# A four-layer graph network on one core: the start re-ordered, the last z kept on chip, the last part spread over four engines

## The chip, the cores and the metric

One core of a Trainium2 chip. The time is device microseconds (us) of one execution, the median of several; most executions of a kernel agree within 0.3%. "The profile" is one execution recorded by the hardware profiler; stages are compared by when their first or last TensorE record starts, read to 0.1 us, so that a difference can be 0.1 off. TensorE does the matrix products and writes them to PSUM, one of the two on-chip memories; the other is SBUF. VectorE, ScalarE and GpSimd do the element-wise work, SyncE and GpSimd issue most transfers.

## The reference

Four graph layers on x of shape (128, 128, 256) in fp32: 128 graphs of 128 nodes, 256 features. Every layer ends in a layer norm over the features.

```python
# _L0: edge attention; _L1: three graph convolutions 256->512->1024->256; _L2: three products
x = _layernorm(x + _L0_gnn_ref(x, ...))
x = _layernorm(x + _L1_gnn_ref(x, ...))
x = _layernorm(x + _L2_gnn_ref(x, ...))
# _L3, cut to what matters: batch norms over ALL 128*128 rows
h   = relu(_batchnorm(agg.reshape(-1, d) @ W1.T + b1, g1, be1))   # z before the norm: 512 wide
out = _batchnorm(h @ W2.T + b2, g2, be2)
x = _layernorm(x + out.reshape(b, n, -1))
```

A batch norm over all rows is a barrier: no row can pass it before the last row's statistics are there. There are two, so the kernel has a loop (layers 0 to 2 and the first product of layer 3), then the second product (the last stage), then the last part (second batch norm applied, addition, layer norm, store).

## The kernel before

The 128 graphs are taken as 32 quads of four. A start fills the software pipeline, a loop runs the quads, and two blocks follow. z (1 MB per quad) and x3, the input of the last addition, are parked in DRAM.

```python
# start (cut): issue order is program order
nc.sync.dma_start(w1_sb, ...)
nc.sync.dma_start(att_dram[0]..., zero)            # 1 MB of zeros
nc.sync.dma_start(w2_sb, ...)                      # 2 MB
...                                                # project quad 0, store its rows
quads[0].xr = load_x(0, "xr", 3, wk)               # 0.5 MB
...                                                # sort the edge index
nc.sync.dma_start(att_dram[1]..., zero)            # 1 MB of zeros
for c in range(NE): score(0, c)                    # score reads the gathered rows
gather(1, [...])                                   # GpSimd: rows of quad 1
... attention(0); scatter(0)                       # GpSimd: attention to DRAM, then loaded back
... stage_a(0)                                     # py: first products with the attention matrix
score(1, NE - 1); values_in(3, xg3); ... softmax of quad 1 ...
attention(1); scatter(1)
mix1(0, 0); mix1(0, 2); first(0, ...); mix2(0, ...)
```

```python
# the end of the loop, and after it (cut)
if c == K3 - 1:
    nc.sync.dma_start(z_dram[k], s.zt...)          # every z goes to DRAM
...
for q in range(NQ):                                # last stage
    z = wk.tile([P, K3, QB * N], F32, tag="zl", bufs=4)
    nc.sync.dma_start(z, z_dram[q]...)
    ... ReLU of the batch norm on ScalarE, 16 matmuls, statistics ...
for q in range(NQ):                                # last part
    nc.sync.dma_start(x3, x3_dram[q]...)
    for o in range(DC): nc.scalar.activation(ag[:, o, :], ...)      # scale and shift
    for j in range(0, QB, 2):
        ... four transposes on TensorE into PSUM ...
        nc.vector.tensor_add(x3[:, j:j + 2, :], x3[:, j:j + 2, :], pt)
        layer_norm(wk, x3[:, j:j + 2, :])          # statistics and both applications on VectorE
    nc.scalar.dma_start(out[...], x3)
```

## Time and profile before

3448.07 us median of 3 runs (3447.54 to 3450.75); profiled span 3446.5.

| stage, by the start of TensorE records | us |
|---|---|
| first product with an attention matrix (py) | 81.8 |
| first large matmul (second convolution of quad 0) | 126.4 |
| last product of the loop (hidden) | 3069.7 |
| first product of the last stage (po) | 3080.6 |
| last product of the last stage | 3301.8 |
| end | 3446.5 |

First a window of the last part. Columns: stretch, its length, then busy us and instructions of TensorE, its weight loads, VectorE, ScalarE and GpSimd, then the granted TensorE clock, the DMA share and GB/s.

```profile
3350.00:3360.00 10.00, 5.31 (x23) 4.17 (x21) 10.00 (x40) 7.76 (x14) 0.00 (x0) 0.50 0.83 254
```

VectorE is full, GpSimd unused, and TensorE at half clock. Then GpSimd's order of events in the start: the gather of quad 1's rows and the first two scatters of quad 0's attention (start, duration, what; in brackets how long the engine had waited, and for what).

```profile
46.62 0.97 POOL L184 DMA_INDIRECT z<-qd,src_idx  x1 [0.30 <-issue]
...
64.16 1.02 POOL L240 DMA_INDIRECT attd<-at,att_idx  x1 [3.97 <-DVE at L234]
67.97 1.01 POOL L240 DMA_INDIRECT attd<-at,att_idx  x1 [2.80 <-DMA attd<-at,att_idx]
```

And TensorE in the end of the start:

```profile
98.46 1.02 PE L206 MATMUL pe<-ident,es 128*16 128x128 f32 x4 [7.36 <-DVE es L199]
99.27 9.58 PE L168 MATMUL pq<-wqv,xt 128*128 128x512 f32 x16
...
111.57 3.50 PE L284 MATMUL pm<-wt_t,xr 128*128 128x128 f32 x16
```

A wait of 7.36 us for edge scores stands ahead of all further work.

### The profile page before, as it was taken

Reading aid. Unit: us, or ns where it says so; the run is one execution under the profiler, and the core shown is the slowest. Engines: PE = TensorE matmul, PEld = TensorE weight load, DVE = VectorE, ACT = ScalarE, POOL = GpSimd, SP = SyncE. Lnnn points to the kernel's source line nnn. Section 1 sums busy time; section 2 is a strip of 40 time slices with the busy share of each in tenths; the row PEclk is TensorE's granted clock in tenths of the full one; section 3 lists DMA queues with packets and bytes.
Section 4 is the critical chain, followed back from the end, with each engine's and each line's share of the span. In section 5 each row is a group of like instructions: output and inputs, shape, how many; then the busy total and the mean of one; then the engine's idle time right before and its main releaser. Section 6 shows DMA issues by size and latency. Waiting matters only on the chain.

```text
span 3446.5 us, 33811 instructions
## 1 busy us (share of the span) xinstructions
PE 3294.4 (96%) x13134; PEld 2102.9 (61%) x13134; DVE 1754.5 (51%) x3522; ACT 979.9 (28%) x1655; POOL 570.1 (17%) x463
## 2 busy tenths in 40 slices
PE   5899999999999999999999999999999999989963
PEld 3566666666666666666666666666666666654442
DVE  6554455544555455455554455545545553233379
ACT  2222222222222222222222222222222222224452
POOL 4211122222221111112122222211111220000000
PEclk7899999999999999999999999999999999999975
DMA  8412333333332322233333333233223331034446
GB/s 259 124 63 73 92 98 99 98 98 86 98 98 80 98 87 79 74 86 98 98 99 98 86 98 98 82 97 90 81 71 87 95 92 37 19 140 163 155 140 220
DMA packets 128015, 348.04 MB, mean 101 GB/s; under 512 B 14576, under 2 KB 68720, under 8 KB 115312
## 3 DMA queue, kind: packets, MB, share of 16 engines
q0 software_dynamic: 41088, 135.29, 16.6%
q1 hardware_dynamic: 65168, 191.58, 15.4%
q10 hardware_dynamic: 21600, 19.02, 1.7%
q8 instruction: 103, 1.69, 0.2%
q14 instruction: 56, 0.46, 0.0%
HBM read 258.82 MB, written 87.03 MB: 100 GB/s over the span
## 4 chain that ended last, share of the span: by engine, by line
PE 93%; DVE 4%; DMA 2%; issue 0%; ACT 0%; POOL 0%; DVEq 0%; POOLq 0%; ACTq 0%; SPq 0%
PE ph L318 26%; PE p L329 13%; PE po L377 10%; PE po L736 6%; PE ph L416 6%; PE ph L298 6%; PE pq L168 6%; PE po L273 3%; PE pm L308 3%; PE pm L363 3%; PE py L264 2%; PE pm L284 2%; PE pa L402 2%; PE po L340 2%; DVE x3l L98 1%; DVE x3l L755 1%
## 5 line engine op out<-in xcount | busy, mean ns | idle before, releaser
L318 PE MATMUL ph<-m,w 128*128 128x512 f32 x2048 | 884.2, 592 | 0.8 <-DVE m L309 0.8
L318 PEld LDWEIGHTS ph<-m,w 128*128 128x128 f32 x2048 | 389.0, 190 | 477.1 <-issue 474.5
L329 PE MATMUL p<-w,h 128*128 128x256 f32 x2048 | 450.4, 381 | 0.0
L184 POOL DMA_INDIRECT zs<-qd,src_idx x124 | 149.9, 1209 | 1729.6 <-DMA qd<-qt 1677.2
L329 PEld LDWEIGHTS p<-w,h 128*128 128x128 f32 x2048 | 386.6, 190 | 52.6 <-issue 0.5
L377 PE MATMUL po<-l2w,ms 128*128 128x256 f32 x1536 | 347.5, 379 | 1.2 <-DVE ms L369 1.2
L321 ACT ACTIVATE h<-ph 128x512 f32<-128x512 f32 x256 | 152.8, 597 | 592.6 <-PE ph L318 592.6
L377 PEld LDWEIGHTS po<-l2w,ms 128*128 128x128 f32 x1536 | 284.3, 190 | 36.1 <-DVE ms L369 1.4
L298 PE MATMUL ph<-w,mx 128*128 128x512 f32 x512 | 235.6, 593 | 0.0
L168 PE MATMUL pq<-wqv,xt 128*128 128x512 f32 x512 | 230.5, 603 | 2.2 <-ACT xt L156 2.2
L736 PE MATMUL po<-zl,l3w 128*128 128x512 f32 x512 | 221.8, 596 | 10.4 <-ACT zl L731 10.4
L416 PE MATMUL ph<-ag,l3w 128*128 128x512 f32 x512 | 225.5, 593 | 0.3 <-ACT ag L405 0.3
L184 POOL DMA_INDIRECT zs<-qd,dst_idx x124 | 192.5, 1553 | 143.8 <-DMA zs<-qd,src_idx 130.1
L342 DVE TENSOR_TENSOR xr<-xr,po 128x512 f32<-128x512 f32 x64 | 43.7, 683 | 338.3 <-PE po L340 338.3
L90 ACT ACTIVATE ln_sd<-ln_mv,eps 128x2 f32<-128x2 f32 x256 | 75.4, 294 | 461.9 <-DVE ln_mv L85 456.7
L240 POOL DMA_INDIRECT attd<-at,att_idx x128 | 128.2, 1001 | 417.9 <-DMA attd<-at,att_idx 283.9
L156 DVE COPY xt<-pt 128x512 f32<-128x512 f32 x58 | 37.4, 686 | 279.9 <-PE pt L154 279.9
L736 PEld LDWEIGHTS po<-zl,l3w 128*128 128x128 f32 x512 | 97.9, 191 | 134.3 <-issue 110.8
L416 PEld LDWEIGHTS ph<-ag,l3w 128*128 128x128 f32 x512 | 96.8, 190 | 121.7 <-issue 112.4
L98 DVE TENSOR_SCALAR xr<-xr,ln_mv,ln_rs 128x256 f32<-128x256 f32 x384 | 163.2, 467 | 6.9
L168 PEld LDWEIGHTS pq<-wqv,xt 128*128 128x128 f32 x512 | 96.5, 194 | 112.6 <-issue 109.1
L309 DVE COPY m<-pm 128x512 f32<-128x512 f32 x128 | 88.3, 690 | 147.2 <-PE pm L308 147.2
(176 smaller groups left out, 4013.9 us busy)
## 6 DMA issues: line engine op xcount, KB each, us to landing
ad<-attd SPq DMA_DIRECT2D x32, 1024.0 KB, 4.8
zd<-z SPq DMA_DIRECT2D x32, 1024.0 KB, 7.9
zl<-zd SPq DMA_DIRECT2D x32, 1024.0 KB, 4.8
xg<-in_x_dram SPq DMA_DIRECT2D x32, 512.0 KB, 4.4
xr<-in_x_dram SPq DMA_DIRECT2D x32, 512.0 KB, 5.8
x3d<-xr SPq DMA_DIRECT2D x32, 512.0 KB, 2.9
x3l<-x3d SPq DMA_DIRECT2D x32, 512.0 KB, 4.9
out_dram<-x3l ACTq DMA_DIRECT2D x32, 512.0 KB, 3.4
```

The lines of the kernel that those rows point to most:

```text
L98: nc.vector.tensor_scalar(r[:, i, :], r[:, i, :], mv[:, i, 0:1], rs[:, i:i + 1], op0=ALU.subtract, op1=ALU.mult)
L168: nc.tensor.matmul(pq, s.xts[i // 2][:, i % 2, c, :], wqv[:, c, :], start=(c == 0), stop=(c == DC - 1))
L184: nc.gpsimd.indirect_dma_start(out=s.z[c], out_offset=None, in_=s.qd, in_offset=bass.IndirectOffsetOnAxis(ap=idx[:, c:c + 1], axis=0), com ...
L240: nc.gpsimd.indirect_dma_start(out=ad, out_offset=bass.IndirectOffsetOnAxis(ap=att_idx[:, c:c + 1], axis=0), in_=s.at[:, c, :], in_offset= ...
L273: nc.tensor.matmul(po[:, t, :], yts[j // 2][:, t, dc, :], wo[:, dc, :], start=(dc == 0), stop=(dc == DC - 1))
L298: nc.tensor.matmul(ph, s.mx[i // 2 * 2][:, i % 2, dc, :], w1_sb[:, dc, :], start=(dc == 0), stop=(dc == DC - 1))
L318: nc.tensor.matmul(ph, w2_sb[:, c, f * P:(f + 1) * P], s.m2[:, c].rearrange("p b n -> p (b n)"), start=(c == 0), stop=(c == K1 - 1))
L321: nc.scalar.activation(h.rearrange("p b n -> p (b n)"), ph, AF.Relu)
L329: nc.tensor.matmul(p3[:, t * D:(t + 1) * D], s.h2[f][:, j + t, :], w3_sb[:, f, :], start=(f == 0), stop=(f == K2 - 1))
L377: nc.tensor.matmul(po[:, i % 2, :], mss[i][:, t, dc, :], l2w[:, t, dc, :], start=(n3 == 0), stop=(n3 == 3 * DC - 1))
L416: nc.tensor.matmul(ph, l3w1[:, dc, c * P:(c + 1) * P], s.ag[:, dc, :], start=(dc == 0), stop=(dc == DC - 1))
L736: nc.tensor.matmul(po, w2t[:, c, o * P:(o + 1) * P], z[:, c, :], start=(c == 0), stop=(c == K3 - 1))
```

## The change

Three intents. **Start:** three loads (w2, one xr, one zero fill, 3.5 MB) are issued later so that the first gather is not stuck behind them, and independent feed-forward work is put ahead of the softmax of quad 1. **Seam:** the last quad's z stays on chip over the first batch norm and is used first, while the other z come in; loads of small constants move to GpSimd. **Last part:** VectorE gives away what others can do. ScalarE applies the layer norm, for half the rows straight from PSUM. For these rows TensorE also does the scaling (a product with a diagonal matrix) and adds x3 (a product with the identity); GpSimd adds the shift to those x3 rows ahead of it and issues the stores.

```diff
-            nc.sync.dma_start(w2_sb, ...)                    # in the head of the start
-            quads[0].xr = load_x(0, "xr", 3, wk)
...
+            xg3 = load_x(3, "xg", 2)                         # behind the second index sort
+            nc.sync.dma_start(w2_sb, ...)
+            quads[0].xr = load_x(0, "xr", 3, wk)
             nc.sync.dma_start(att_dram[1]..., zero)
-            xg3 = load_x(3, "xg", 2)
... end of the start: values of quad 3 first, then score(1), mixes, first(0, 0) between the
... softmax steps of quad 1, and attention(1), scatter(1) last
... loop's last pass: third_mix between the halves of third; aggregation by halves
-            if c == K3 - 1:
+            if k == NQ - 1:
+                kept["z"] = s.zt
+            elif c == K3 - 1:
                 nc.sync.dma_start(z_dram[k], ...)
...
     with ExitStack() as phase:
+        bufs = phase.enter_context(tc.tile_pool(name="bufs", bufs=1))   # 14 large buffers
         cst = phase.enter_context(tc.tile_pool(name="cst3", bufs=1))    # constants
...
-            nc.scalar.dma_start(t, ap...)                    # b, gamma, beta
+            nc.gpsimd.dma_start(t, ap...)
...
+        order = [NQ - 1] + list(range(NQ - 1))
... last part, per quad
+                nc.scalar.activation(ag[:, o, :2 * N], ...)             # two, halves only
+                nc.gpsimd.tensor_add(x3s[q][:, 2:, :], x3s[q][:, 2:, :], shift_bc...)
+                        if j < 2: nc.tensor.transpose(...)
+                        else:     nc.tensor.matmul(dst_ps, a_in, diag2[:, o, :], ...)
+                nc.tensor.matmul(pt[1], ident, x3s[q][:, 2:, :], start=False, stop=True)
+                    mvs[q] = wk.tile([P, QB, 2], F32, tag="mv3", ...)   # mean and variance
+                    nc.vector.tensor_add(x3s[q][:, :2, :], x3s[q][:, :2, :], sums[q][0])
+                nc.vector.scalar_tensor_tensor(nm, mvs[q][:, :, 0], -1.0, rs, ...)  # the product
+                for i in range(QB): nc.scalar.activation(x3s[q][:, i, :], src_, ...)
+                nc.gpsimd.dma_start(out[...], x3s[q])
```

More of the change, by code (lines that the diff above doesn't have):

```diff
@@ L75, in gnn_stack @@
     st1 = ctile([P, K3, NQ, 6], "st1")
+    zpool = ctx.enter_context(tc.tile_pool(name="zpool", bufs=1))
+    kept = {}
     def norm_stats(pool, r):
@@ L322, in second, with third @@
             s.h2.append(h)
-        def third(k, j):
+        def third(k, j, between=None):
             s = quads[k]
@@ L327, in third @@
             for t in range(2):
+                if t and between:
+                    between()
                 for f in range(K2):
@@ L398, in stage_f @@
             ag = wk.tile([P, DC, QB * N], F32, tag="ag", name="ag", bufs=1)
-            for dc in range(DC):
-                pa = ps("pa")
-                for i in range(QB):
-                    nc.tensor.matmul(pa[:, i * N:(i + 1) * N], s.xr[:, i, dc * P:(dc + 1) * P], ahat_t,
+            pas = [ps("pa") for _ in range(DC)]
+            for i0, dc in ((i0, dc) for i0 in range(0, QB, 2) for dc in range(DC)):
+                for i in (i0, i0 + 1):
+                    nc.tensor.matmul(pas[dc][:, i * N:(i + 1) * N], s.xr[:, i, dc * P:(dc + 1) * P], ahat_t,
                                      start=True, stop=True)
+            for dc, pa in enumerate(pas):
                 if dc == 0:
@@ L412, in hidden @@
             if c == 0:
-                s.zt = wk.tile([P, K3, QB * N], F32, tag="z", name="z", bufs=1)
+                s.zt = zpool.tile([P, K3, QB * N], F32, tag="z", name="z", bufs=1)
             ph = ps("ph3")
@@ L475, in iteration @@
                 third(c, 0)
-                third(c, 2)
-                third_mix(c, 0)
                 if has_b:
+                    third(c, 2)
+                    third_mix(c, 0)
                     mix1(b, 0)
-                third_norm(c, 0)
+                    third_norm(c, 0)
+                else:
+                    third(c, 2, lambda: third_mix(c, 0))
+                    third_norm(c, 0)
                 third_mix(c, 2)
@@ L527, in start @@
                                         accum_out=rank[:, c:c + 1])
-            perm = wk.tile([P, NE, E], F32, tag="m2", name="perm", bufs=1)
+            perm = w2_sb[:, :2, :].rearrange("p c f -> p (c f)").rearrange("p (c e) -> p c e", c=NE)
             for c in range(NE):
@@ L541, in start @@
             nc.sync.dma_start(att_dram[0][:N * N, :].rearrange("(t s) r -> t (s r)", s=N), zero)
-            nc.sync.dma_start(w2_sb, w2.rearrange("(c p) f -> p c f", p=P))
             values_in(0, xg0, nc.scalar.copy)
@@ L596, in start @@
                 nc.vector.tensor_scalar(rs, kp, 1.0, BIG, op0=ALU.subtract, op1=ALU.mult)
+            xg3 = load_x(3, "xg", 2)
+            nc.sync.dma_start(w2_sb, w2.rearrange("(c p) f -> p c f", p=P))
+            quads[0].xr = load_x(0, "xr", 3, wk)
             nc.sync.dma_start(att_dram[1][:N * N, :].rearrange("(t s) r -> t (s r)", s=N), zero)
-            xg3 = load_x(3, "xg", 2)
             for c in range(NE):
@@ L605, in start @@
                     nc.vector.tensor_copy(log_col, pc[:, :, 1])
-            z2 = wk.tile([P, 2, QB * D], F32, tag="z", name="z_1", bufs=1)
+            z2 = zpool.tile([P, 2, QB * D], F32, tag="z", name="z_1", bufs=1)
             gather(1, [z2[:, 0, :], z2[:, 1, :], wk.tile([P, QB * D], F32, tag="xb", name="xb_1", bufs=1),
@@ L665, in start @@
             stage_a(0)
+            values_in(3, xg3)
+            for i in range(QB):
+                values(3, i)
             score(1, NE - 1)
-            values_in(3, xg3)
-            steps = softmax_parts(1)
-            for i in range(QB):
-                next(steps)
-                values(3, i)
-            for _ in steps:
-                pass
-            attention(1)
-            scatter(1)
             mix1(0, 0)
             mix1(0, 2)
+            steps = softmax_parts(1)
             first(0, 0)
+            next(steps)
             for i in range(QB):
@@ L682, in start @@
                 mix2(0, i)
+                next(steps, None)
+            attention(1)
+            scatter(1)
         with tc.manual_schedule(engines=None):
@@ L696, in vec @@
             t = ctile([P, n], name, pool=cst)
-            nc.scalar.dma_start(t, ap.rearrange("(c p) -> p c", p=P))
+            nc.gpsimd.dma_start(t, ap.rearrange("(c p) -> p c", p=P))
             return t
+        b1, g1, be1 = (vec(n, ap, K3) for n, ap in (("b1", l3_b1), ("g1", l3_g1), ("be1", l3_be1)))
         w2t = ctile([P, K3, D], "l3w2", pool=cst)
-        nc.scalar.dma_start(w2t, l3_w2_t.rearrange("(c p) f -> p c f", p=P))
-        b1, g1, be1 = (vec(n, ap, K3) for n, ap in (("b1", l3_b1), ("g1", l3_g1), ("be1", l3_be1)))
+        nc.gpsimd.dma_start(w2t, l3_w2_t.rearrange("(c p) f -> p c f", p=P))
         b2, g2, be2 = (vec(n, ap, DC) for n, ap in (("b2", l3_b2), ("g2", l3_g2), ("be2", l3_be2)))
@@ L724, in gnn_stack @@
         sc1, sh1 = batch_norm(st1, K3, b1, g1, be1, "n1")
-        outs = []
-        for q in range(NQ):
-            z = wk.tile([P, K3, QB * N], F32, tag="zl", name="zl", bufs=4)
-            nc.sync.dma_start(z, z_dram[q].rearrange("p (c n) -> p c n", c=K3))
-            for c in range(K3):
-                nc.scalar.activation(z[:, c, :], z[:, c, :], AF.Relu, bias=sh1[:, c:c + 1], scale=sc1[:, c:c + 1])
-            ag = keep.tile([P, DC, QB * N], F32, tag=f"agg{q}", name=f"agg{q}")
-            for o in range(DC):
-                po = ps("po3")
-                for c in range(K3):
-                    nc.tensor.matmul(po, w2t[:, c, o * P:(o + 1) * P], z[:, c, :],
-                                     start=(c == 0), stop=(c == K3 - 1))
-                nc.vector.bn_stats(st2[:, o, q, :], po)
-                nc.vector.tensor_copy(ag[:, o, :], po)
-            outs.append(ag)
@@ L741, in gnn_stack @@
-        sc2, sh2 = batch_norm(st2, DC, b2, g2, be2, "n2")
-        for q in range(NQ):
-            x3 = wk.tile([P, QB, D], F32, tag="x3", name=f"x3l{q}", bufs=7)
-            nc.sync.dma_start(x3, x3_dram[q].rearrange("p (b d) -> p b d", b=QB))
-            ag = outs[q]
-            for o in range(DC):
-                nc.scalar.activation(ag[:, o, :], ag[:, o, :], AF.Identity, bias=sh2[:, o:o + 1],
-                                     scale=sc2[:, o:o + 1])
-            for j in range(0, QB, 2):
-                pt = ps("pt3").rearrange("p (b d) -> p b d", d=D)
-                for t in range(2):
-                    for o in range(DC):
-                        nc.tensor.transpose(pt[:, t, o * P:(o + 1) * P], ag[:, o, (j + t) * N:(j + t + 1) * N], ident)
-                nc.vector.tensor_add(x3[:, j:j + 2, :], x3[:, j:j + 2, :], pt)
-                layer_norm(wk, x3[:, j:j + 2, :])
-            nc.scalar.dma_start(out[q * QB:(q + 1) * QB].rearrange("b n d -> n b d"), x3)
+        NB = 14
@@ new lines, in buf, with load_z @@
+        def buf(name):
+            return bufs.tile([P, 2 * QB * N], F32, tag="buf", name=name, bufs=NB)
+        def load_z(q):
+            if q == NQ - 1:
+                return [kept["z"][:, 2 * h:2 * h + 2, :] for h in range(2)]
+            z = [buf(f"zl{q}_{h}").rearrange("p (c n) -> p c n", c=2) for h in range(2)]
+            zq = z_dram[q].rearrange("p (c n) -> p c n", c=K3)
+            for h in range(2):
+                nc.sync.dma_start(z[h], zq[:, 2 * h:2 * h + 2, :])
+            return z
@@ new lines, in gnn_stack, with spread, load_x3, scaled @@
+        order = [NQ - 1] + list(range(NQ - 1))
+        outs = {}
+        with tc.manual_schedule(engines=None):
+            for q in order:
+                z = load_z(q)
+                for c in range(K3):
+                    zc = z[c // 2][:, c % 2, :]
+                    nc.scalar.activation(zc, zc, AF.Relu, bias=sh1[:, c:c + 1], scale=sc1[:, c:c + 1])
+                ag = keep.tile([P, DC, QB * N], F32, tag=f"agg{q}", name=f"agg{q}", bufs=1)
+                for o in range(DC):
+                    po = ps("po3")
+                    for c in range(K3):
+                        nc.tensor.matmul(po, w2t[:, c, o * P:(o + 1) * P], z[c // 2][:, c % 2, :],
+                                         start=(c == 0), stop=(c == K3 - 1))
+                    nc.vector.bn_stats(st2[:, o, q, :], po)
+                    nc.vector.tensor_copy(ag[:, o, :], po)
+                outs[q] = ag
+            sc2, sh2 = batch_norm(st2, DC, b2, g2, be2, "n2")
+            diag2 = ctile([P, DC, P], "diag2", pool=cst)
+            shift_bc = ctile([P, D], "shift_bc", pool=cst)
+            ones = ctile([P, P], "ones3", pool=cst)
+            nc.gpsimd.memset(ones, 1.0)
+            def spread():
+                wide = ctile([P, DC, P], "wide", pool=cst)
+                for o in range(DC):
+                    nc.vector.tensor_scalar(wide[:, o, :], ident, sh2[:, o:o + 1], None, op0=ALU.mult)
+                    nc.vector.tensor_scalar(diag2[:, o, :], ident, sc2[:, o:o + 1], None, op0=ALU.mult)
+                pr = ps("shift_ps")[:, :D]
+                nc.tensor.matmul(pr, ones, wide.rearrange("p o n -> p (o n)"), start=True, stop=True)
+                nc.vector.tensor_copy(shift_bc, pr)
+            x3s, sums, mvs, coefs = {}, {}, {}, {}
+            def load_x3(q):
+                x3s[q] = buf(f"x3l{q}").rearrange("p (b d) -> p b d", b=QB)
+                nc.sync.dma_start(x3s[q], x3_dram[q].rearrange("p (b d) -> p b d", b=QB))
+            def scaled(q):
+                ag = outs[q]
+                for o in range(DC):
+                    nc.scalar.activation(ag[:, o, :2 * N], ag[:, o, :2 * N], AF.Identity, bias=sh2[:, o:o + 1],
+                                         scale=sc2[:, o:o + 1])
+                if q == 0:
+                    spread()
+                nc.gpsimd.tensor_add(x3s[q][:, 2:, :], x3s[q][:, 2:, :], shift_bc.unsqueeze(1).to_broadcast([P, 2, D]))
+                pt = [ps("pt3").rearrange("p (b d) -> p b d", d=D) for _ in range(2)]
+                for j in range(QB):
+                    for o in range(DC):
+                        dst_ps, a_in = pt[j // 2][:, j % 2, o * P:(o + 1) * P], ag[:, o, j * N:(j + 1) * N]
+                        if j < 2:
+                            nc.tensor.transpose(dst_ps, a_in, ident)
+                        else:
+                            nc.tensor.matmul(dst_ps, a_in, diag2[:, o, :], start=(j == 2 and o == 0), stop=False,
+                                             skip_group_check=True)
+                nc.tensor.matmul(pt[1], ident, x3s[q][:, 2:, :], start=False, stop=True, skip_group_check=True)
+                sums[q] = pt
+            def moments(q, half):
+                if half == 0:
+                    mvs[q] = wk.tile([P, QB, 2], F32, tag="mv3", name="mv3", bufs=3)
+                    moments.st = wk.tile([P, QB, 6], F32, tag="st3", name="st3", bufs=2)
+                    nc.vector.tensor_add(x3s[q][:, :2, :], x3s[q][:, :2, :], sums[q][0])
+                src_ = x3s[q][:, :2, :] if half == 0 else sums[q][1]
+                for t in range(2):
+                    nc.vector.bn_stats(moments.st[:, 2 * half + t, :], src_[:, t, :])
+                for t in range(2):
+                    nc.vector.bn_aggr(mvs[q][:, 2 * half + t, :], moments.st[:, 2 * half + t, :])
+            def coefficients(q):
+                rs = wk.tile([P, QB], F32, tag="rs3", name="rs3", bufs=2)
+                nm = wk.tile([P, QB], F32, tag="nm3", name="nm3", bufs=2)
+                nc.vector.reciprocal(rs, coefs[q])
+                nc.vector.scalar_tensor_tensor(nm, mvs[q][:, :, 0], -1.0, rs, op0=ALU.mult, op1=ALU.mult)
+                coefs[q] = (rs, nm)
+            def apply(q):
+                rs, nm = coefs[q]
+                for i in range(QB):
+                    src_ = x3s[q][:, i, :] if i < 2 else sums[q][1][:, i - 2, :]
+                    nc.scalar.activation(x3s[q][:, i, :], src_, AF.Identity, bias=nm[:, i:i + 1], scale=rs[:, i:i + 1])
+                nc.gpsimd.dma_start(out[q * QB:(q + 1) * QB].rearrange("b n d -> n b d"), x3s[q])
+            for q in range(NB - 1):
+                load_x3(q)
+            scaled(0)
+            for q in range(NQ + 1):
+                if q < NQ:
+                    moments(q, 0)
+                if q + 1 < NQ:
+                    scaled(q + 1)
+                if q > 0:
+                    coefficients(q - 1)
+                    apply(q - 1)
+                    if q + NB - 2 < NQ:
+                        load_x3(q + NB - 2)
+                if q < NQ:
+                    moments(q, 1)
+                    sd = wk.tile([P, QB], F32, tag="sd3", name="sd3", bufs=2)
+                    nc.scalar.activation(sd, mvs[q][:, :, 1], AF.Sqrt, bias=eps)
+                    coefs[q] = sd
```

## The prediction

> **What bounds the kernel now.** I read the page's busy slices first, then the list of who waited for whom on TensorE, then the chain that ended last, then the ends of the span in small windows and instruction by instruction.
>
> ```profile
> PE   5899999999999999999999999999999999989963
> DVE  6554455544555455455554455545545553233379
> PEclk7899999999999999999999999999999999999975
> ```
>
> Forty slices of 86 us. TensorE is full from about slice 3 to slice 37, at full clock: that is the loop over quads (93.2 us each in the chain) and the first half of layer 3 (221.8 us for 512 matmul records). The diff changes none of those matmuls, so some 3200 of 3446 us cannot move. Only the ends can: the first slice and a half, the seam near 3070 us, and the last slice and a half, where VectorE is full and TensorE is not.
>
> ```profile
> PE pt L754 <- DVE ln_mv L85: 47.9, 22, 2.2
> PE pe L206 <- DVE es L199: 24.4, 2, 17.0
> PE py L264 <- ACT adc L250: 10.8, 1, 10.8
> PE po L736 <- ACT zl L731: 10.4, 1, 10.4
> PE pa L402 <- DVE xr L98: 2.4, 1, 2.4
> PE pm L363 <- DVE xr L98: 1.8, 1, 1.8
> ```
>
> TensorE's own waits (total us, times, longest): the last part's transposes behind VectorE, two waits for edge scores in the first 100 us (17.0 and 7.4), one for the first attention matrix, one for the first z of the last stage. The other rows of this list are at most 5.5 us.
>
> ```profile
> 3070.89 3.83 DMA zd<-z
> 3074.87 4.76 DMA zl<-zd
> 3080.61 221.80 PE po L736 x512
> ```
>
> The chain at the seam: store the last z, then load z again, then matmuls.
>
> ```profile
> L83 DVE BATCH_NORM_STATS2 ln_st<-x3l 128x6 f32<-128x256 f32 x128 | 50.2, 400 | 0.0
> L748 ACT ACTIVATE agg<-agg,n2shift,n2scale 128x512 f32<-128x512 f32 x64 | 47.5, 799 | 0.8 <-DVE n2shift L721 0.8
> L98 DVE TENSOR_SCALAR x3l<-x3l,ln_mv,ln_rs 128x256 f32<-128x256 f32 x128 | 44.1, 400 | 0.1
> L755 DVE TENSOR_TENSOR x3l<-x3l,pt 128x512 f32<-128x512 f32 x64 | 41.5, 652 | 2.5 <-PE pt L754 2.5
> L85 DVE BATCH_NORM_AGGREGATE ln_mv<-ln_st 128x2 f32<-128x6 f32 x128 | 19.8, 161 | 0.0
> 3427.60 0.15 DVE L85 BATCH_NORM_AGGREGATE ln_mv<-ln_st 128x2 f32<-128x6 f32 x1
> 3431.78 0.15 DVE L85 BATCH_NORM_AGGREGATE ln_mv<-ln_st 128x2 f32<-128x6 f32 x1
> ```
>
> The groups from 3303 us on, and one instruction of the same place in two successive quads: 4.18 us per quad, VectorE never idle. 32 x 4.18 = 134, with some 6 us of batch norm and start and 4 us of last store this is the 144 us from the last matmul (3302.4) to the end.
>
> **What the Trainium skill says.** "ScalarE: Activation LUTs", section What ACT_TABLE_LOAD costs: 186 ns + 0.833 ns per element, 93 ns more for each per-partition pointer operand, and back-to-back instructions overlap by 93 ns. The trace agrees: 186 + 2 x 93 + 427 = 799 ns, and the mean above is 799; three in a row took 2.21 us, so one each 0.705. For 256 columns with scale and bias this gives 585 ns, 492 ns apart (an estimate from that page). "TensorE: Matmul & The Clock Gate", section What's actually happening: the clock halves after an idle window of about 3.4 us and returns after a busy one. The trace agrees: granted clock 0.50 nearly throughout the last part, where TensorE was under 55% busy; 0.77 and then 1.00 just after 3308 to 3312 us, the 4 us in which it was wholly busy. "DMA: Bandwidth & Descriptors", section Issuing engines are not separate DMA queues: all queues share the same 16 engines. In the trace the first store of projected rows landed after 7.1 us beside the weight loads (DMA share about 1.0 from 5 to 30 us), later ones after 2.6.
>
> **The change, part by part.**
>
> Start. Some 3.5 MB (w2 2 MB, one xr 0.5, one zero fill 1) leave the head of the load queue and go behind the second index sort (34 us). At the 376 to 398 GB/s of those windows they took 9 us of all engines. Without them the row store at 15.6 us should land at about 18.3, so the first gather starts at 19 (indices ready at 18.8) rather than 23.5; a gather's landing falls from 6.9 us towards the 4.0 us minimum, and gathers wait for each other in pairs. Four scores of 3.7 us on VectorE then start at 29 and end near 44 rather than 54.7: up to 10 us. But GpSimd issues the second quad's gather ahead of the first scatter, and that gather needs a row store issued at 38 us, into the moved loads. I credit 6 to 8 us, say 7.
>
> End of the start. Values of quad 3 no longer wait for score and softmax of quad 1: TensorE's waits of 7.4 and 1.9 us go. But its copies stand behind the first layer norm on VectorE (about 3 to 4 us between transposes and projections), the score transposes now fall among the mixes, and attention 1 stands ahead of the first large matmuls (about 2 us of waiting for the last scan). Counted along TensorE, 35.3 us from 91.1 to 126.4 becomes about 33: 2 us gained. The scatter of quad 1 comes 14 us later relative to the large matmuls (27.5 us); its rows are needed after them, ScalarE holds up for 8 us in the middle and eight PSUM banks carry that: no loss. Start in all: **9 us**, 5 to 13.
>
> Loop. Unchanged, except its last two passes: third mix between the two halves of the third product hides the 1.8 us wait and some of 1.2 us after it; the re-ordered aggregation puts only four more records (0.5 us) ahead of its 2.4 us wait. **3 us**.
>
> Seam. The last z stays on chip and is used first. The normalisation's shift is ready at 3073.8; one 0.80 us ReLU and the matmuls can start at 3074.7 rather than 3080.6. Other z loads no longer stand behind the store, so they come in under the 6.9 us of the first quad. **6 us**.
>
> Last part, per quad. VectorE: one addition of 512 columns (0.72 until its result can be used), four statistics in pairs (2 x 0.67), four aggregates (2 x 0.2), reciprocal and product (0.2 + 0.1): about 2.75 us against 4.18. ScalarE: two scalings and four applications, 6 x 0.492, and a root every 0.20: **3.15 us**. GpSimd: one addition, 1.27 us by the same shape in the bias row, plus issuing the store (indirect ones cost it 0.95 us, estimate 1 to 2): under 3.3. TensorE: four transposes at 0.117 apart, four matmuls of two records at 0.12, one of 512 columns at 0.86: 2.3 us at full clock, 4.6 at half. So ScalarE becomes the bound at 3.15 if TensorE keeps its clock. The order ties the engines to each other: scaling of a quad, transposes (0.8 to 1.1), VectorE's first half (1.6) and coefficients (0.4) must fit between two applications, 2.9 to 3.2 us in all; and half-clock stretches will cost. I take 3.4 us. Fixed: start 10.8 us (diagonals, broadcast of the shift, one cold round; the last aggregate no longer hidden), end 8 us (apply, issue, land). 10.8 + 31 x 3.4 + 8 = 124 against 144: **20 us**.
>
> Sum: 9 + 3 + 6 + 20 = 38; 3448 - 38 = 3410, and I say **3409**.
>
> **Rivals.** (1) TensorE as the bound of the last part: at half clock its 4.6 us exceed even the old 4.18; then 10.8 + 31 x 4.6 + 8 = 161, 17 us lost rather than 20 gained, total 3447. For it: clock 0.50 there before. Against: 4.6 us of work at a pace of 3.4 makes it wholly busy, which brought the clock back at 3312 us. It may swing; a mean of 3.4 to 3.8 allows for that. (2) VectorE stays the bound and ScalarE hides: 2.75 per quad, last part 104, total about 3390. Against: the activation formula that fits the trace. (3) GpSimd: a store of 512 rows of 1 KB issued by it may cost far more than an indirect one; no such issue is in this trace. Each store stands between two additions, so over 2 us it would set the pace: 4 us per quad gives 143, total 3429. (4) The start gains nothing, since the moved 3.5 MB then collide with the second gather: total 3417. (5) DMA in the last part: 16.8 MB out and some 10 MB in within 105 us is 255 GB/s; it moved 252 to 267 at shares of 0.77 to 0.85 before. Close, not binding.
>
> **Range and chances.** The last part spans about 0 to 32 us gained, the start 5 to 13, seam and loop 7 to 10: 3390 to 3429. Over 2% faster means below 3379, which needs rival 2 and the best start: 0.05. Over 2% slower needs a stage broken: 0.01.
>
> **What would show it.** Second-large-matmul start (126.4 now) near 117 to 118; first matmul of the last stage 4.5 us after the previous one, not 10.4; between successive stores 3.2 to 3.6 us, ScalarE over 85% busy and TensorE's clock above 0.8 there; GpSimd store issue under 2 us. Wrong if the clock stays 0.5, if stores on GpSimd exceed 2 us, or if a loop pass is no longer 93.2 us.

## The result, and the profile after

3427.77 us median (3420.79 to 3429.73, 4 runs), against 3449.41 (3447.54 to 3451.13, 4 runs) of the kernel before beside it: ratio 0.9934, 95% interval 0.9917 to 0.9951, 0.66% faster. Ratios here are the mean time of one kernel's runs over that of the other's of the same rounds, so not quite the ratio of the medians quoted. The profiled spans are 3446.5 and 3425.8.

| stretch (profiled runs) | before | after | gained | predicted |
|---|---|---|---|---|
| to the first py | 81.8 | 88.7 | -6.9 | 7 |
| py to the first large matmul | 44.6 | 39.9 | 4.7 | 2 |
| to the last hidden product | 2943.3 | 2942.4 | 0.9 | 3 |
| last hidden to first po (the seam) | 10.9 | 11.9 | -1.0 | 6 |
| first to last po | 221.2 | 221.3 | -0.1 | 0 |
| last po to the end | 144.7 | 121.6 | 23.1 | 20 |
| sum | 3446.5 | 3425.8 | 20.7 | 38 |

The total lies inside the range, but the two smaller stretches that were to gain 13 us together lost 7.9.

**Last part.** Two windows of the kernel after, same columns as before:

```profile
3340.00:3350.00 10.00, 8.15 (x40) 5.27 (x39) 8.37 (x33) 8.61 (x20) 5.35 (x7) 0.86 0.90 297
3350.00:3360.00 10.00, 9.48 (x52) 5.88 (x51) 9.13 (x35) 10.00 (x24) 6.98 (x7) 1.00 0.88 287
```

ScalarE is full where nothing disturbs (second line) and TensorE has full clock. From one quad's square root on ScalarE to the next it takes 3.06 us there; before, 4.18 a quad. Three quads take 4.43 to 4.77. One of those, over all engines:

```profile
3334.24 1.42 DVE L826 SCALAR_TENSOR_TENSOR nm<-mv,rs 128x4 f32<-128x4 f32 x1
3334.35 1.28 POOL L798 TENSOR_TENSOR x3l<-x3l,shift_bc 128x512 f32<-128x512 f32 x1
...
3335.70 1.09 ACT L833 ACTIVATE x3l<-x3l,nm,rs 128x256 f32<-128x256 f32 x2 [1.50 <-DVE nm L826]
```

VectorE's product of 4 numbers per partition took 1.42 us instead of 0.16. It ended at 3335.66, GpSimd's addition at 3335.63, and ScalarE idled 1.50 us for it.

**Start.** SyncE issues the moved loads at 37 to 39 us; GpSimd then waits for the store of quad 1's rows before it can gather them, and later for its scatters.

```profile
37.05 0.37 SPq L607 DMA_DIRECT2D w<-in_w_dram  x1
37.47 0.52 SPq L120 DMA_DIRECT2D xr<-in_x_dram  x1
38.04 1.01 SPq L609 DMA_DIRECT2D attd<-zero  x1
```

```profile
51.77 2.01 POOL L186 DMA_INDIRECT z<-qd,src_idx  x1 [10.32 <-DMA qd<-qt]
...
67.64 1.02 POOL L242 DMA_INDIRECT attd<-at,att_idx  x1 [0.30 <-issue]
75.81 1.01 POOL L242 DMA_INDIRECT attd<-at,att_idx  x1 [7.14 <-DMA attd<-at,att_idx]
```

The row store was issued at 41.0 us and landed 10.5 us later (before: issued at 38.2, landed 6.5 us later); the gather starts at 51.77 instead of 46.62. The gather ends so late that the first scatter stands behind it on GpSimd ("issue": nothing to wait for), and GpSimd then waits 7.14 us for that scatter's write instead of 2.80. The first gather did start earlier, 20.43 against 23.46, but the last score came at 55.5 against 54.5.

TensorE's own waits between 60 and 132 us (total, times, longest), after:

```profile
PE py L266 <- ACT adc L252: 16.9, 1, 16.9
PE pq L170 <- DVE xt L158: 4.0, 1, 4.0
PE pat L232 <- DVE m L222: 3.0, 2, 2.2
...
PE pe L208 <- DVE es L201: 1.4, 1, 1.4
```

The wait for edge scores fell from 7.4 to 1.4 us as intended, and a wait of 4.0 us for copies on VectorE took its place in part.

**Seam.** The chain that ended last, after:

```profile
3071.64 0.59 ACT z L423
...
3072.33 0.81 POOL b L707
...
3076.80 6.06 DMA be<-in_l_be_dram
...
3082.89 4.32 PE po L762 x5
```

Store and reload of z are gone. In their place stand the loads of six short vectors and a weight, issued by GpSimd one after the other only after the last hidden product: GpSimd's wait for TensorE ends at 3071.65, with that product (the chain names ScalarE's copy of the last z, which ended just ahead of the first load).

### The profile page after: what moved, and what is told of

Its sections match the earlier page's. It is cut to its first block, busy times and chain, and to the rows that moved or that the text cites. A ratio compares the mean times of both kernels' runs of the same rounds, so it can differ in the third digit from the quotient of the medians.

```text
span 3425.8 us, 34423 instructions
## 1 busy us (share of the span) xinstructions
PE 3326.6 (97%) x13328; PEld 2111.0 (62%) x13328; DVE 1715.3 (50%) x3367; ACT 1016.9 (30%) x1751; POOL 641.9 (19%) x535
## 4 chain that ended last, share of the span: by engine, by line
PE 94%; ACT 2%; DVE 2%; DMA 1%; issue 0%; POOL 0%; ACTq 0%; POOLq 0%; DVEq 0%
PE ph L320 26%; PE p L333 13%; PE po L381 10%; PE po L762 6%; PE ph L421 6%; PE pq L170 6%; PE ph L300 6%; PE po L275 3%; PE pm L310 3%; PE pm L367 3%; PE py L266 2%; PE po L344 2%; PE pm L286 2%; PE pa L406 2%; ACT x3l L833 1%; PE pt L372 1%
## 5 line engine op out<-in xcount | busy, mean ns | idle before, releaser
L762 PE MATMUL po<-zl,l3w 128*128 128x512 f32 x496 | 213.0, 592 | 0.0
L92 ACT ACTIVATE ln_sd<-ln_mv,eps 128x2 f32<-128x2 f32 x192 | 56.5, 294 | 388.2 <-DVE ln_mv L87 388.2
L310 PEld LDWEIGHTS pm<-wt_t,h 128*128 128x128 f32 x1024 | 131.8, 191 | 47.7 <-issue 39.9
```

The costliest lines, as they stand in the source:

```text
L310: nc.tensor.matmul(pm[:, c, :], s.h1[i][:, c * P:(c + 1) * P], wt_t, start=True, stop=True)
L762: nc.tensor.matmul(po, w2t[:, c, o * P:(o + 1) * P], z[c // 2][:, c % 2, :], start=(c == 0), stop=(c == K3 - 1))
```

## The experiments

Ten kernels ran, in three groups, each group on one chip beside the kernel before: e1 to e4 (before 3451.07), e5 to e8 (before 3465.54), e9 and e10 (before 3452.41). On the chip of the second group the loop takes some 17 us longer in all four profiles; what causes that was not studied, and I compare stretches outside the loop, and ratios.

What the runs can tell apart: the kernel after was not run in the first two groups, and the ratio intervals of e1 to e4 and e6 to e8 all overlap its own (0.9917 to 0.9951), so by total time none of these edits is told from it; only e5 and e9 are. The single effects below are read from one profile each. How far such readings repeat can be seen where an edit did not touch a stage: the last part is 121.3 to 121.6 us in six profiles, the seam 11.8 to 12.2 in seven, py starts at 87.6 to 89.6 and the first large matmul at 127.2 to 128.9 in six.

**e1: constants placed before the large buffers.** In the built program, the pool opened first takes the lowest addresses. Opening the 14 buffers (56 KB per partition) first pushes the small constants up, across the end of the loop's pool of working tiles and into the start of its pool of weights. They lie over no weight of the last hidden product, but the wait that the build puts ahead of the first load is for that product, which reads another weight of the same pool. Before, the constants lay over a pool that was last read at 3063 us. Theory: memory. Rival: loads issued by GpSimd are slow.

```diff
-        bufs = phase.enter_context(tc.tile_pool(name="bufs", bufs=1))
         cst = phase.enter_context(tc.tile_pool(name="cst3", bufs=1))
+        bufs = phase.enter_context(tc.tile_pool(name="bufs", bufs=1))
```

> Changed kernel with the two pools of the last phase opened in the other order (the small constants first, the buffer pool second), so that the batch-norm vectors and moments no longer lie over memory that the last large weights of the loop occupy. Theory (memory reuse): the vector loads and the first aggregates then wait only for the aggregation matmuls, the gap of TensorE between the last loop matmul and the first matmul of the last stage falls from 11.3 us to about 4.5 us, total about 3421. Rival (the loads are slow because GpSimd issues them, 6 us from issue to landing each): the loads start some 8 us earlier but the aggregates still come late, gap 8 us or more, total 3424 or more.

3422.06 us (3419.69 to 3426.37), ratio 0.9926 (0.9912 to 0.9939). The chain at the seam:

```profile
3072.20 1.03 DVE n1mv L720
...
3074.24 0.17 DVE n1shift L731
...
3074.50 0.82 ACT z L757
...
3075.37 10.98 PE po L762 x21
```

Start to start, the seam is 5.2 us instead of 11.9: 6.7 back, and it is now the batch norm's own arithmetic. The loads still come from GpSimd, now issued from 3064 to 3068 us and landing after 2.5 to 3.8 us (after: from 3072 to 3077, 5.8 to 7.7), so the rival falls. The swap also has the loads of z start 6.6 us later, at 3070.9, and no longer beside them; the two effects were not taken apart. Two swapped lines, which change no operation, were worth more than the store and reload of z that they hid.

**e2: the moved loads back in their old places,** and with them the permutation of the index sort, which the change had put into the memory of w2, back in its own buffer. All else as changed.

```diff
-            nc.sync.dma_start(w2_sb, ...)   # after the second sort; xr and zero fill likewise
+            nc.sync.dma_start(w2_sb, ...)   # in the head of the start, as before
```

> Changed kernel with the three moved loads of the start (w2, first xr, second zero fill) back in their old places and the permutation back in its old buffer; the new order of the end of the start is kept. Theory (the moved loads delay the row store of quad 1, thus its gather and the first scatter, by 7 us): the first attention rows are back near 81.8 us, the first large matmuls start near 122 instead of 128.7, total about 3421. Rival (the new order of the end of the start costs the time, the loads do not matter): the large matmuls still start near 128, total 3427.

3426.32 us (3422.34 to 3427.10), ratio 0.9931 (0.9917 to 0.9944). py starts at 84.1 (after: 88.7), the first large matmul at 123.6 (128.6). So 4.6 us at py and 5 at the first large matmul come back when the loads do not move, less than the 7 expected, and the total does not show them (ratio 0.9931 against 0.9934). The second gather starts at 48.73. That py is still 2.3 us later than before goes with the clock: TensorE's last group of products for quad 1 took 6.32 us (8 records, half clock) against 3.68 before, and the row store was issued at 41.8 us instead of 38.2.

**e3: the moved loads later still**, w2 behind the scatter of quad 0, the zero fill just ahead of it (a zero fill still later shares a buffer with the attention rows and deadlocks in the build).

```diff
-            nc.sync.dma_start(w2_sb, ...)
             quads[0].xr = load_x(0, "xr", 3, wk)
-            nc.sync.dma_start(att_dram[1]..., zero)
...
+            nc.sync.dma_start(att_dram[1]..., zero)
             scatter(0)
+            nc.sync.dma_start(w2_sb, ...)
```

> Changed kernel with w2 loaded only after the first attention rows, and the second zero fill just ahead of the first scatter, so neither runs beside the gathers of quads 0 and 1. Theory (DMA contention): the row store of quad 1 lands in about 3 us instead of 10.5, the second gather starts near 43 instead of 52, the large matmuls start near 118, total about 3417. Rival (GpSimd's in-order issue of gather and scatter sets the pace): second gather no earlier than 50, total 3425 to 3428.

3423.17 us (3420.07 to 3424.40), ratio 0.9921 (0.9908 to 0.9935). GpSimd's gather of quad 1 and the first two scatters:

```profile
44.16 1.83 POOL L186 DMA_INDIRECT z<-qd,src_idx  x1 [2.34 <-DMA qd<-qt]
...
60.91 1.02 POOL L242 DMA_INDIRECT attd<-at,att_idx  x1 [2.69 <-DVE at L236]
67.26 1.00 POOL L242 DMA_INDIRECT attd<-at,att_idx  x1 [5.33 <-DMA attd<-at,att_idx]
```

The gather now starts 7.6 us earlier than after and 2.5 earlier than before; the first scatter starts 3.3 us earlier than before. But GpSimd waits 5.33 us for its write instead of 2.80. The zero fill, issued at 64.24, may be what falls on it; but the DMA share is already 1.06 from 60 to 64 us, while quad 1's own gathers land, so that this cause is not shown. py starts at 82.1, as before. The last score ends at 51.2 us, 3.3 earlier than before. The first large matmul starts at 120.7, not at the 118 expected, 7.9 us earlier than after; by 242.2 only 5.1 of it are left (after: 247.3), because TensorE ran this block at half clock:

```profile
120.00:126.00 6.00, 5.87 (x11) 2.74 (x12) 5.20 (x7) 0.00 (x0) 2.73 (x2) 0.50 0.01 1
```

The same six us of the kernel after (128.6 to 134.6) had clock 1.00, with the same 2.2 us idle just ahead of them.

**e4: mean and variance kept in PSUM.** Theory: the product of two SBUF inputs is held up by GpSimd's addition, which reads SBUF. The Trainium skill, "SBUF — State Buffer", section Who interferes with whom, says that a VectorE instruction with two SBUF inputs contends with a GpSimd instruction that reads SBUF and that the second to issue blocks until the first is done. If so, putting one input in PSUM (in a bank already emptied) takes the wait away and leaves the work as it is. Rival: the long periods come from half-clock stretches of TensorE, and the long products are only a symptom.

```diff
-                    mvs[q] = wk.tile([P, QB, 2], F32, tag="mv3", name="mv3", bufs=3)
...
                     nc.vector.tensor_add(x3s[q][:, :2, :], x3s[q][:, :2, :], sums[q][0])
+                    mvs[q] = sums[q][0][:, 0, :2 * QB].rearrange("p (b t) -> p b t", t=2)
```

> Changed kernel with mean and variance of the last layer norm kept in the PSUM bank that the first addition has emptied, so the coefficient product has one SBUF input and one PSUM input instead of two SBUF inputs. Theory (VectorE's product is held while GpSimd's addition runs, three or so times, 1.3 to 1.9 us instead of 0.16): no such instruction over 0.3 us, ScalarE's waits for it go from 6.7 us to under 3, last part from 121 to about 117 us, total about 3424. Rival (the long periods come from half-clock stretches of TensorE and the long products are a symptom): last part within 1.5 us of 121.

3422.65 us (3421.96 to 3423.96), ratio 0.9923 (0.9910 to 0.9937). The product in the kernel after, then in e4 (count, then shortest, median and longest ns, first and last start):

```profile
L826 DVE SCALAR_TENSOR_TENSOR nm<-mv,rs x32: 161/163/1880, 3318.5 to 3418.2; 128x4 f32<-128x4 f32 x32
```

```profile
L826 DVE SCALAR_TENSOR_TENSOR nm<-pt,rs x32: 160/163/164, 3317.5 to 3413.0; 128x4 f32<-128x4 f32 x32
```

The long ones are gone, and it is not that the two no longer meet. Twice in e4 a product starts while an addition runs, and takes 0.16 us all the same; this is one of them:

```profile
3333.17 1.28 POOL L798 TENSOR_TENSOR x3l<-x3l,shift_bc 128x512 f32<-128x512 f32 x1
3333.33 0.16 DVE L826 SCALAR_TENSOR_TENSOR nm<-pt,rs 128x4 f32<-128x4 f32 x1
```

So the trace agrees with the page that the two instructions get in each other's way and that one input outside SBUF ends it; the rival falls. Which of the two goes first the records do not tell: each of the three long products ended 0.03 us after an addition, but one had started 0.40 us into it, one 0.11 us ahead of it (the case shown above) and one, of 1.88 us, 0.57 us ahead of it.

The last part is 4.2 us shorter (121.6 to 117.4), but the held product is not all of that. Some 1.3 us come from a second effect of the edit: ScalarE's square root now reads PSUM, the next instruction starts 0.147 us after it instead of 0.188, and the undisturbed period falls from 3.06 to 3.01. The other 2.9 come from the long quads, which are shorter but not gone (3.70 and 3.76 us for two of them).

**e5: the three repairs together.**

```diff
+ e1 (pool order), e3 (loads late), e4 (mean and variance in PSUM)
```

> The three repairs together: small constants placed before the large buffers (alone it gave a seam gap of 4.6 us instead of 11.3), the large loads and zero fill issued later in the start (alone first large matmul 120.7 instead of 128.6 us, of which 5.1 us were left at 242 us), and the moments of the last part written to the emptied PSUM bank (alone 4.2 us off the last part). Theory: they lie in three separate stretches of the execution, so they add: 5 + 6.7 + 4.2 = 16 us under the changed kernel, so a profiled span of about 3410 us and a ratio to the kernel before of 0.989. Rival: the last part is also limited by the transfers, or the earlier stretches only shift waits, and less than 10 us of it remain (over 3416 us).

3426.66 us (3426.09 to 3428.39) on the slower chip, ratio 0.9889 (0.9873 to 0.9906), as expected by ratio. Seam 5.2, last part 117.3, first large matmul at 121.4: the parts add. This time the large block ran at full clock and its end kept all 7.3 us (240.0 against 247.3).

**e6: one of four normalisations on GpSimd**, on top of e4, to ask what paces the last part.

```diff
                 for i in range(QB):
+                    if i == 0:
+                        nc.gpsimd.tensor_scalar(x3s[q][:, i, :], src_, rs[:, i:i + 1], nm[:, i:i + 1],
+                                                op0=ALU.mult, op1=ALU.add)
+                        continue
```

> On top of the moments in PSUM, the first of the four normalisations of every quad in the last part is done by GpSimd instead of ScalarE. Theory A (ScalarE is what paces the last part, 9.8 to 10 us busy in 10): ScalarE's work falls by about a quarter and VectorE, 9.3 us busy in 10 at a period of 3.01 us, sets the pace next: period 2.75 to 2.85, last part 109 to 113 us instead of 116.8, span 3413 to 3417. Rival B (the DMA queues pace it, 0.98 to 1.00 of their time at 350 GB/s in part of that stretch): period stays at 2.95 to 3.05, ScalarE shows 8 of 10 us busy, last part 115 to 118. Rival C (GpSimd's extra 256-column operation costs over 1 us and its addition, operation and store issue then exceed 3 us): period above 3.05 and a longer last part.

3438.89 us (3435.60 to 3442.55), ratio 0.9927 (0.9910 to 0.9943). The last part is 113.8 us against e4's 117.4. A window of e4, then two of e6:

```profile
3370.00:3380.00 10.00, 9.23 (x46) 5.45 (x46) 9.55 (x38) 10.00 (x24) 7.01 (x8) 1.00 1.00 352
```

```profile
3385.00:3395.00 10.00, 9.16 (x46) 5.23 (x44) 9.55 (x38) 8.96 (x21) 8.57 (x11) 1.00 0.99 363
...
3405.00:3415.00 10.00, 9.27 (x47) 5.43 (x45) 9.55 (x37) 9.05 (x22) 8.56 (x11) 1.00 0.56 193
```

ScalarE falls to 9.0 of 10, so it did pace. But the undisturbed period falls only from 3.01 to 2.95, not to the expected 2.75 to 2.85: VectorE's sequence (one addition, four statistics, four aggregates, reciprocal, product) takes 2.95 us with no idle between its instructions, and 9.55 of 10 is what full looks like there. Of these 2.95 us e4's edit adds 0.2: two aggregates take 0.40 us when they write to PSUM, 0.30 in the kernel after. The pace is the same with the DMA share at 0.99 and at 0.56, so transfers do not set it, though by the period alone rival B would have fitted. Only 2 us of the 3.6 come from the pace (31 x 0.06), the rest from shorter start-up and long periods.

**e7: z stored and loaded again**, with e1's pool order: what is keeping z worth?

```diff
-            if k == NQ - 1:
-                kept["z"] = s.zt
-            elif c == K3 - 1:
+            if c == K3 - 1:
...
-        order = [NQ - 1] + list(range(NQ - 1))
+        order = list(range(NQ))
```

> The kernel with the small constants first, but the last quad's z is stored and loaded again like the other 31 and the quads run in the order 0 to 31, so this measures what keeping z is worth. Theory: the first load of z can start only when the memory of the loop's last work is free (the first one was issued at 3070.9 us with the small constants first) and takes 3 us or more to land, its ReLU and then the matmul follow: seam gap 7 to 10 us instead of 4.6, total 3 to 5 us longer than with the small constants first alone (3422), so 3425 to 3427. Rival: the load lands before the batch norm's scale is ready anyway, and nothing changes (gap under 5.5 us).

3442.18 us (3437.68 to 3446.11), ratio 0.9934 (0.9918 to 0.9951). The gap itself is nearly the same, 6.0 us start to start against 5.2: half a z lands in time. The price comes just after it. TensorE's waits at the seam (total, times, longest), then the chain:

```profile
PE po L758 <- ACT zl L753: 7.0, 2, 5.5
```

```profile
3090.10 8.85 DMA zl<-zd
...
3098.97 0.82 ACT zl L753
...
3099.84 4.73 PE po L758 x6
```

The second half is 8.85 us under way; of the 7.0 us of waiting 5.5 are the gap itself and 1.5 come in the middle of the first quad. So interrupted, TensorE stays at half clock longer: granted 0.50 from 3095 to 3100 us and 0.63 from 3100 to 3105, where e1 has 0.69 from 3076 to 3081 and then 1.00. From the last hidden to the last po it is 230.9 us against e1's 226.3: 0.8 in the gap, 1.5 in the second wait, and some 2.3, the rest, in slower matmuls. So keeping z is worth 4.6 us at the seam, within what the theory gave, but its step "the gap is 7 to 10" was wrong: TensorE's wait of 5.5 us is what the rival named (under 5.5), and looking at the gap alone would have called the kept z worthless. In the last part e7 is 2.7 us faster than e1, 1.6 of it because only two quads meet the long period (4.68, 4.69) instead of three: another order of quads moves the collisions. Net, about 2 us, which the totals (0.9934 against 0.9926, intervals overlapping) cannot confirm.

**e8: the end of the start in its old order**, all else as changed.

```diff
+            score(1, NE - 1); values_in(3, xg3); ... softmax; attention(1); scatter(1)
             mix1(0, 0)
             ...
-            attention(1); scatter(1)
```

> The changed kernel with the order of the end of the start (values of quad 3, scores, softmax, attention and scatter of quad 1 ahead of the first feed-forward work) as it was before; everything else as changed. Theory: the re-ordering is worth what the traces showed between the attention stage and the first large matmul, 44.6 to 39.9 us, so with the attention stage at 88 to 89 us the first large matmul starts at 132 to 134 us instead of 128.6, and the total is 4 to 5 us longer, about 3432. Rival: the shorter distance only made up for the later start of the attention stage (the scores of quad 1 had more time to finish), and the first large matmul starts within 1.5 us of 128.6.

3446.14 us (3445.59 to 3446.98), ratio 0.9945 (0.9928 to 0.9962). py starts at 88.0 and the first large matmul at 129.9: 41.9 us, against 39.9 after and 44.6 before. So the order is worth 2.0 us, not 4.7 (the other profiles with the new order have 38.4 to 39.9). Where the other 2.7 come from:

```profile
104.98 1.02 PE L208 MATMUL pe<-ident,es 128*16 128x128 f32 x4 [7.35 <-DVE es L201]
105.80 8.04 PE L170 MATMUL pq<-wqv,xt 128*128 128x512 f32 x16
...
116.44 2.05 PE L286 MATMUL pm<-wt_t,xr 128*128 128x128 f32 x16
```

The wait for scores is the same 7.35 us as before. But the two groups that took 9.58 and 3.50 us before take 8.04 and 2.05: 3.0 us, with the same instructions in the same order. The granted clock in the ten us from 108.2 was 1.00, in the same place before (from 102) 0.84. My expectation's first theory took the whole difference of two traces for the worth of the order; its rival had the number right (129.9 is within 1.5 us of 128.6) but named another cause than the one found.

**e9 and e10: all four edits, and the changed kernel again as its control.**

```diff
+ e9: e1, e3, e4 and e6 together        e10: no edit
```

> The three repairs of the combined kernel and one of four normalisations per quad on GpSimd. Theory: the last part is limited by VectorE once ScalarE is relieved, as in the run that had this alone (113.2 us from the last matmul record of the stage before, against 116.8), and this stretch does not depend on the repairs elsewhere: 3.6 us under the combined kernel, ratio to the kernel before about 0.988, and 21 to 23 us under the changed kernel run on the same chip. Rival: the transfers then fill 0.97 or more of the last part and hold it at 116 us or more, so the ratio stays at 0.989.

> The changed kernel itself, unedited, on the same chip as the kernel with all four edits, as its control and to see how the measured ratio of 0.9934 holds on another chip. Theory: the ratio does not depend on the chip: 0.9925 to 0.9945. Rival: the two chips differ in the loop only, a constant some 15 us in both kernels, and the difference in us, 21 to 22, is what holds rather than the ratio (these two differ by under 0.0001, so this run cannot tell them apart).

e9: 3408.47 us (3406.14 to 3409.72), ratio 0.9875 (0.9860 to 0.9890). e10: 3427.52 (3427.06 to 3429.10), ratio 0.9933 (0.9920 to 0.9947), as on the first chip. e9 beats both kernels, by 19.1 us under the changed one instead of the expected 21 to 23. By stage (against the profile of the kernel after, same span as e10's): 3.3 us up to the last hidden product, 6.7 at the seam, 0.4 in the last stage, 8.0 in the last part. The shortfall is in the first: the large matmuls started 7.3 us earlier, but the block up to the first hidden product again took 121.4 us (118.7 after), as in e3, with some matmul records at twice their time, and the rest of the loop 1.3 us more.

## Why the prediction was right or wrong

- **Total:** 3409 predicted, 3427.77 measured, in the range of 3390 to 3429 and "same", as was most likely. The gain was 21.6 us where 39 was predicted, so the total is inside by 1.2 us only, with the start and the seam wrong in sign: that it fell inside is as much luck as insight.
- **Last part, 20 us: right in mechanism, 23.1 measured.** ScalarE became the bound and TensorE got its full clock, so rivals 1 and 2 did not happen; GpSimd's store issue took 0.76 to 0.79 us, so rival 3 did not. Term by term, 10.8 + 31 x 3.4 + 8 was measured, from the end of the last matmul, as 11.9 + 31 x 3.26 + 8.1. ScalarE's 3.15 us a quad is 3.06 where nothing disturbs, and VectorE's 2.75 fits (2.76 when the starts of its instructions are added up without idle; e6's 2.95 is that of another kernel). The allowance of 0.25 over ScalarE's 3.15 was put down to engines that depend on each other and to half clock. The 31 periods exceed 31 x 3.06 by 6.2 us, and 4.7 of these lie in the three quads in which VectorE's product is held by GpSimd's addition; without that hold (e4) the excess is 2.9 us less.
- **Start, 7 us from the moved loads: wrong, 6.9 lost.** The step that failed is "up to 10 us ... I credit 6 to 8". The prediction saw the collision with the second gather, but took it for a discount and, in rival 4, for the loss of the whole gain, no more. In fact the row store was issued 2.8 us later than before (the first of quad 1's two groups of products ran in part at half clock, 5.40 us against 3.70) and took 10.5 us instead of 6.5; the gather began 5 us later, stood ahead of the first scatter, and py was 6.9 us late. e2 (loads back: 4.6 us) and e3 (loads later: 6.6 us at py) show the moved loads as the cause of most of it. The credit itself was mis-sized too: the scores were to start at 29 us and end near 44, since a gather's landing would fall from 6.9 us towards 4.0. They started at 33.2 and ended at 55.5, and in e3, with none of the moved loads but xr beside the gathers, at 34.2 and 51.2, the gathers of quad 0 landing after 4.8 to 9.2 us: 3.3 us are gained there, not 10. At py nothing is left of them (82.1), since the scatters then wait longer.
- **End of the start, 2 us: right, though the traces showed 4.7.** e8 gives 2.0 for the order; the rest goes with the clock granted to two groups of matmuls. The Trainium skill, "TensorE: Matmul & The Clock Gate", section What's actually happening, calls the window free-running, so that the point of transition depends on where in it the work lands; half clock in e3's first large block and full clock in e5's, with equal code up to there, agrees with that. So does the clock record of all twelve profiles: every stretch of one granted clock that begins and ends inside a profile lasts a whole multiple of 3.41 us. Of the same wait of 2.2 us ahead of the large block, 1.6 us (e3) and 1.5 us (e9) lay in the stretch of 3.41 us before the clock halved; where it stayed full it was split more evenly (1.2 us in e5, 1.3 after). No rule for how much idle time it takes follows from that: other such stretches with less work kept the full clock.
- **Loop, 3 us: 0.9 measured.** The stretch is 2942.3 or 2942.4 us in the profiles of the kernel after, e1, e4 and e10, and 2943.3 in that of the kernel before. No run takes the two re-orderings apart, but TensorE's waits in the last passes do. Before they are 1.8 us (pm), 1.2 (ms) and 2.4 (pa), as the prediction lists and names them, 5.4 in all. After, the first is gone, but a new one of 0.7 us stands ahead of it, the second is 1.3, the third has lost the 0.5 us credited, and ScalarE's copies of the aggregate add 0.5: 4.4 in all. So the step that failed is that the re-ordered third mix hides the 1.8 us and some of the 1.2.

```profile
PE pa L406 <- DVE xr L100: 1.9, 1, 1.9
PE po L381 <- DVE ms L373: 1.3, 1, 1.3
PE po L344 <- ACT s L336: 0.7, 1, 0.7
PE ph L421 <- ACT ag L410: 0.5, 2, 0.2
```

- **Seam, 6 us: wrong, 1.0 lost; its mechanism is right.** The step that failed is "the normalisation's shift is ready at 3073.8". It was ready 6 us later, because its vectors could not be loaded earlier: the order in which two pools were opened had put them into a pool still in use. The weight of the first product, loaded behind the vectors, landed later still, at 3082.3. With the pools swapped (e1), last hidden to last po falls from 232.1 before to 226.3: 5.8 of the 6, of which keeping z gives 4.6 (e7).
- **Readings and sums of the prediction that do not hold.** The list of TensorE's waits leaves out a row of 10.5 us (the last part's transposes behind ScalarE's scaling, 6 times), so "the other rows are at most 5.5 us" is wrong. Of the stores of projected rows "later ones" did not all land after 2.6 us: the next, quad 1's, took 6.5. That the trace agrees with a clock halved by an idle window of about 3.4 us is not shown: in the last part before, TensorE never waited longer than 2.24 us after 3308 us, and yet the clock fell to half at 3319.7 and stayed there, and in e3 the clock halved 1.6 us into a wait. The ends of the range are not the sums of the parts given for it (12 to 55 us gained, 3393 to 3436).

## What to carry to other kernels

A load moved out of one wait's way lands in another's: before moving it, list every small transfer on the latency path that falls into its new time, and count the loss as well as the missing gain. When a block of large buffers is added, look at which earlier pool each small constant now lies over, since here the last read of that pool decided when its load could start. Price a re-ordering by undoing it alone: the difference of two traces also holds clock phases and collisions that have nothing to do with it.

## What the Trainium skill lacked or had wrong

- "SBUF — State Buffer", section Who interferes with whom: that the two instructions contend, and that a VectorE instruction with one SBUF input does not, is as stated (e4), but the page gives no size for the smallest instructions. Here a product of 4 elements per partition took 0.91 to 1.88 us instead of 0.16 three times in 32, and the last part lost 2.9 us by it. That whoever issues first goes first is not what the records show: in one of the three cases the product's record starts 0.57 us ahead of the addition's and ends 0.03 us after it.
- No page that I read ties the order in which memory is allotted to the time a load may be issued: swapping two lines changed the seam from 11.9 to 5.2 us.
- No page that I read sizes what bulk loads do to short transfers beside them: the store of quad 1's projected rows landed after 10.5 us beside the moved loads, after 6.5 in the start before and after 3.6 in e3; in the loop such a store takes 2.6.
